# Channel attention and a non-local block on one core: layer 1 taken two steps at a time, and four smaller edits beside it

## The chip, the cores and the metric

One Trainium2 chip, of which the kernel uses one core: TensorE (PE), VectorE (DVE), ScalarE (ACT), GpSimd (POOL), and the queues that issue transfers (SyncE, SP, and GpSimd's own). The metric is the device time of one execution in microseconds (us). Everything is computed in float32 except for a few bf16 helpers, and a 512-column float32 matmul shows in the trace as two records.

## The reference

Two images of 256 channels and 64 x 64 = 4096 positions go through two layers.

```python
# layer 0, per image: attention between positions, 8 heads of 32 channels
q, k, v = split(w_qkv @ x)
scores = q^T k / sqrt(32)                 # 4096 x 4096 per head
x = w_proj @ (softmax(scores) v) + x

# layer 1, per image: a non-local block
g   = maxpool2(g_w @ x + g_b)             # 256 x 1024
th  = theta_w @ x[:64] + theta_b          # 64 x 4096
phi = maxpool2(phi_w @ x[64:] + phi_b)    # 64 x 1024
y   = softmax(th^T phi) g^T               # softmax over the 1024 pooled positions
out = batchnorm(W_w @ y + W_b) + x
```

## The kernel before

The order of stages is: q, k and v of image 0; `attend(0)`, which is layer 0's attention, in 2 quads of heads times 8 blocks of 512 positions; `project(0)`; `non_local(0)`, which is layer 1; and the same three for image 1. Softmax subtracts the true maximum of every row, so each block of scores is computed twice: once for its maxima (`ps` in layer 0, `f` in layer 1), once for the exponentials (`s` in layer 0, `f2` in layer 1, whose tile shows as `f` at L816 too). The maxima of later blocks run between the steps of the present one, one piece with each call of `advance`.

**Denominators of layer 0.** The exponentials `p` of a block are summed over its 32 key steps in three places: two heads in `sums[0]`, by GpSimd additions (L517, L526), the other two in `sums[1]` and `sums[2]`, by accumulating transfers that GpSimd issues (L523, 1 MB each). `normalize` is a generator that the code after it advances in pieces. For most blocks GpSimd folds the sums and the matmuls with `ones` (L544, tile `den`) add over the partitions. For the last block of an image, matmuls add all the pieces instead: `sums[0]`, in image 1 also `blk.last` (which VectorE accumulates, L515), and four halves of `sums[1]` and `sums[2]`. ScalarE copies `den` to `r`, VectorE takes the reciprocal (L555), and GpSimd multiplies the numerators `y` by it (L581). `project` works through eight blocks of 512 columns with four matmuls each (L646, two buffers of the pool `ps_s`), and VectorE adds the residual x, loaded by SP into `x_res`, into `y` (L653). It runs all of `normal` out before its block 4.

**Layer 1.** `ps_s` has two buffers of two PSUM banks (`scores`), `ps_m` four of one bank (`scratch`). For each block i of 512 columns, theta and the first half of phi are row-tiled matmuls (64 rows each, L683 and L684, at the same time in two parts of the array), the second half of phi is a full 128-row matmul (L687). ScalarE writes theta with its bias, VectorE pools phi. Then g follows in two halves (L703), each pooled by VectorE (L710). The recording layer `tc` may let an instruction of later code stand earlier on its engine; `tc.issue_after(x)` holds the instructions recorded under it behind x. In the built program the matmuls of `wg` (W applied to g, L725) stand between the two halves of g in blocks 1 to 7. After that come six pieces of maxima, and the loop over 8 blocks of 4 steps: `f2` (L816, two row-tiled matmuls, and at step 0 also the negated maxima, L827), exp on ScalarE (L831), then `weigh` of the step before: four full matmuls (L778) into two `scratch` banks and GpSimd's additions of p for the denominator. One piece of maxima (`f`, L746, two row-tiled matmuls and one VectorE reduce over 1024 elements, L753) follows each step. When a block's maxima are complete, GpSimd splits them into three bf16 terms (L141 to L145), TensorE turns them (`pt`, L150) and ScalarE copies them to `rows` (L161). At the end of a block `result` runs a `den` matmul (L790), reads it through ScalarE into `r` (in block 7 the reciprocal reads `den` in PSUM), takes the reciprocal, and VectorE makes z from the two y banks in four steps (L798, L801); one transfer per block stores z.

The buffers of tag `one` (six of 128 x 1024) hold p of both layers, `x_res`, `whole` and z.

Of the kernel before, what the change touches and what calls it, by code (L numbers as in the profile page):

```python
# [35 lines left out]
def conv_attention(  # L36
# [393 lines left out]
    def attend(b, y):  # L430
# [97 lines left out]
        def normalize(blk):  # L528
            theirs = [blk.sums[n][:, j] for j in range(2) for n in (1, 2)]
            if (blk.qd, blk.i) != (QUADS - 1, NI - 1):  # L530
                with tc.issue_after(added.ins):
                    nc.gpsimd.dma_start(out=blk.sums[1], in_=blk.sums[2], accum_op=ALU.add)
                yield
                theirs = [single(f"whole_{blk.name}")]
                with tc.issue_after(added.ins):
                    nc.gpsimd.tensor_add(theirs[0], blk.sums[1][:, 0], blk.sums[1][:, 1])
                yield
            den = scratch(f"den_{blk.name}")
            mine = [[blk.sums[0], *blk.last], theirs]
            for n in range(max(map(len, mine))):  # L540
                for h in range(QH):
                    those = mine[h // 2]
                    if n < len(those):
                        nc.tensor.matmul(  # L544
                            den[bass.ts(h, D), :],
                            ones[:, :D],
                            those[n][:, h % 2, :],
                            start=(n == 0),
                            stop=(n == len(those) - 1),
                        )  # L550
            r = work.tile([P, NB], F32, tag="r", name=f"r_{blk.name}", bufs=1)
# [84 lines left out]
    def project(b, y, normal, wproj_sb):  # L636
        for i in range(NI):
            if i == NI // 2:
                for _ in normal:
                    pass  # L640
            cols = bass.ts(i, NB)
            xc = load_x(b, i, single(f"x_res_{b}_{i}"))
            s = scores(f"proj_{b}_{i}")
            for o in range(NC):
                for c in range(NC):
                    nc.tensor.matmul(  # L646
                        s[:, o, :],
                        wproj_sb[:, c, bass.ts(o, P)],
                        y[:, c, cols],
                        start=(c == 0),  # L650
                        stop=(c == NC - 1),
                    )
            nc.vector.tensor_add(y[:, :, cols], s, xc)  # L653
# [4 lines left out]


    def non_local(b, y, theta_w, phi_w):  # L660
        theta = [double(f"theta_{b}_{t}") for t in range(2)]
# [14 lines left out]
        nc.sync.dma_start(out=ww_sb, in_=ww.rearrange("(o p) m -> p o m", p=P))  # L676
        for i in range(NI):
            cols, small = bass.ts(i, NB), bass.ts(i, NB // 4)
            s = scores(f"tp_{b}_{i}")
            with ExitStack() as order:  # L680
                if i:
                    order.enter_context(tc.issue_after(last_g.ins))
                nc.tensor.matmul(s[:, 0, :], theta_w, y[:CM, 0, cols], start=True, stop=True)  # L683
            nc.tensor.matmul(  # L684
                s[:, 1, :], phi_w[CM:, 0, :], y[CM:, 0, cols], start=True, stop=False
            )
            nc.tensor.matmul(s[:, 1, :], phi_w[:, 1, :], y[:, 1, cols], start=False, stop=True)  # L687
            nc.scalar.activation(
                theta[i], s[:, 0, :], AF.Identity, bias=par[:, THETA_B : THETA_B + 1]
            )  # L690
            nc.vector.tensor_reduce(
                phi[:, small].rearrange("p (r w) -> p r w", w=WW // 2),
                pooled(s[:, 1, :]),
                AX.XY,
                ALU.max,
            )
            nc.vector.tensor_scalar_add(
                phi[:, small], phi[:, small], par[:, PHI_B : PHI_B + 1]
            )
            s = scores(f"g_{b}_{i}")  # L700
            for o in range(NC):
                for c in range(NC):
                    last_g = nc.tensor.matmul(  # L703
                        s[:, o, :],
# [13 lines left out]
                )  # L718
        nc.gpsimd.tensor_sub(dphi, phi[:, 2 * P :], phi[:, : M - 2 * P])

        for t in range(M // P // 2):
            a = scratch(f"wg_{b}_{t}")
            for j in range(2):
                for c in range(NC):
                    nc.tensor.matmul(  # L725
                        a[:, bass.ts(j, C)],
# [7 lines left out]
            )  # L734

        ready = []

        def maxima1():
            for i in range(NI):
                neg = work.tile([P, NB // P, QH], F32, tag="neg1", name=f"neg1_{b}_{i}")  # L740
                nc.gpsimd.memset(neg, 0.0)
                for g in range(NB // P):
                    f = scores(f"f_{b}_{i}_{g}")
                    for h in range(2):
                        half = bass.ts(h, CM)
                        nc.tensor.matmul(  # L746
                            f[:, h, :],
                            theta[i][half, bass.ts(g, P)],
# [3 lines left out]
                        )  # L752
                    nc.vector.tensor_reduce(neg[:, g, 0:1], f, AX.XY, ALU.max, negate=True)  # L753
                    if g < NB // P - 1:
                        yield
                nc.vector.tensor_copy(neg[:, :, 2], neg[:, :, 0])
                ready.append(negate(f"l1_{b}_{i}", neg, 1))
# [5 lines left out]
        last = M // P // 2 - 1  # L763
        acc, waiting = {}, None

        def weigh(i, t, p):
            if t == 0:
# [3 lines left out]
            else:  # L771

                for j in range(2):
                    nc.gpsimd.tensor_add(acc[i][NC], acc[i][NC], p[:, j, :])  # L774
            for j in range(2):
                edge = dict(start=(t == 0 and j == 0), stop=(t == last and j == 1))
                for o in range(NC):
                    nc.tensor.matmul(  # L778
                        acc[i][o], wg[:, 2 * t + j, bass.ts(o, P)], p[:, j, :], **edge
                    )  # L780
            if t == last:
                finish.append(i)

        finish = []

        def result(i):
            cols = bass.ts(i, NB)
            z = single(f"z_{b}_{i}")
            den = scratch(f"den1_{b}_{i}")
            nc.tensor.matmul(den, ones, acc[i][NC], start=True, stop=True)  # L790
            r = work.tile([P, NB], F32, tag="r", name=f"r1_{b}_{i}", bufs=1)
            if i < NI - 1:

                nc.scalar.copy(r, den)
                den = r
            nc.vector.reciprocal(r, den)  # L796
            for o in range(NC):
                nc.vector.scalar_tensor_tensor(  # L798
                    z[:, o, :], acc[i][o], bn_scale[:, o : o + 1], r, ALU.mult, ALU.mult
                )  # L800
                nc.vector.scalar_tensor_tensor(  # L801
                    z[:, o, :], z[:, o, :], bn_shift[:, o : o + 1], y[:, o, cols], ALU.add, ALU.add
                )
            nc.sync.dma_start(out=dst[:, :, cols], in_=z)

        advance(maxes1, NB // P + 2)
        later = ready[0]()
        for i in range(NI):
            rows = later
            for t in range(last + 1):  # L810
                if t == 0:
                    s = scores(f"f2_{b}_{i}")
                for h in range(2):
                    half = bass.ts(h, CM)
                    keys = phi if t == 0 else dphi[:, 2 * P * (t - 1) :]
                    nc.tensor.matmul(  # L816
                        s[:, h, :],
                        keys[half, bass.ts(h, P)],
                        theta[i][half, :],
                        start=(t == 0),  # L820
                        stop=(t > 0),
                        skip_group_check=t > 0,
                    )
                for h in range(2):
                    half = bass.ts(h, CM)
                    if t == 0:
                        nc.tensor.matmul(  # L827
                            s[:, h, :], ones_b[half, :], rows[half, :], start=False, stop=True
                        )
                p = single(f"p1_{b}_{i}_{t}")  # L830
                nc.scalar.activation(p, s, AF.Exp)  # L831
                if waiting is not None:
                    weigh(*waiting)
                waiting = (i, t, p)
                if finish:
                    result(finish.pop())
                if t == last and i + 1 < NI:
                    later = ready[i + 1]()
                advance(maxes1)
        weigh(*waiting)  # L840
        result(finish.pop())


# [87 lines left out]
```

## Time and profile before

| | us |
|---|---|
| median of 3 runs | 3885.74 (3884.22 to 3887.61) |
| the profiled execution, whole time | 3884.94 |
| its span | 3883.1 |
| `project` of image 0, start of its first full run to the first theta matmul | 1728.43 to 1760.23 |
| layer 1 of image 0, first theta matmul to end of the last `den` | 1760.23 to 2006.1 |
| `project` of image 1 (its first two records stand at 3594.55) | 3596.61 to 3627.18 |
| layer 1 of image 1 to the end of the span | 3627.18 to 3883.1 |

A page of the profile gives each engine's busy time and share, then the chain of work that ended last, by engine and line. A row of the chain is: start, length, engine, tile, line, records. A row of the timeline is: start, length, engine, line, operation, tiles written and read, their shapes, count; in brackets how long the engine had been idle before it, and what ended the wait. Records that stand for one group overlap in time, so pace is read from starts, not from a record's length. `SPq` and `POOLq` are queues that issue transfers.

### The profile page before, as it was taken

To read this page: it belongs to the slowest core of one execution; us is meant where nothing else is said; L and a number is where in the kernel's file an instruction comes from. 1 tells how busy PE (TensorE), PEld (TensorE's weight loads), DVE (VectorE), ACT (ScalarE), POOL (GpSimd) and SP (SyncE) were. 2 spreads that over 40 slices of the span, in tenths; PEclk is the share of its full clock that TensorE was granted. 3 is DMA by queue.
4 is the path that set the end of the run, shared out by engine and by line. 5 is a ranking of instruction groups with operands and counts; after the bars stand their busy time and mean duration, and the time that the engine had idled before them with its cause. 6 is when DMAs were issued, how large, how long until landed. Compare 5 with 4: busy or idle time off the path is not lost.

```text
span 3883.1 us, 69996 instructions
## 1 busy us (share of the span) xinstructions
PE 3852.5 (99%) x27452; PEld 1361.3 (35%) x27452; DVE 2898.4 (75%) x5449; ACT 2702.5 (70%) x3386; POOL 3092.8 (80%) x1959
## 2 busy tenths in 40 slices
PE   9999999999999999999999999999999999999998
PEld 4333333333333333333333333333333333332333
DVE  5888888788888888774458888888888888884444
ACT  5787777777777787761237777777778888887121
POOL 1888899899888999891448899998999999997043
PEclk9999999999999999999999999999999999999999
DMA  1778878778888788880018888887788888889200
GB/s 58 147 167 169 171 165 170 167 166 172 167 169 165 167 167 171 170 193 15 22 40 167 168 176 168 173 171 164 162 186 170 169 169 170 169 166 187 65 17 27
DMA packets 112876, 567.31 MB, mean 146 GB/s; under 512 B 20264, under 2 KB 22568, under 8 KB 51360
## 3 DMA queue, kind: packets, MB, share of 16 engines
q0 software_dynamic: 68832, 501.25, 63.9%
q1 hardware_dynamic: 43024, 60.79, 4.6%
q8 instruction: 215, 3.52, 0.3%
q14 instruction: 117, 0.96, 0.1%
q10 hardware_dynamic: 688, 0.79, 0.1%
HBM read 51.63 MB, written 8.88 MB: 16 GB/s over the span
## 4 chain that ended last, share of the span: by engine, by line
PE 96%; DMA 2%; POOL 1%; DVE 1%; issue 0%; ACT 0%; DVEq 0%; POOLq 0%; ACTq 0%
PE s L460 27%; PE w L484 26%; PE ps L301 23%; PE y L778 6%; PE q L197 2%; PE k L197 2%; PE f L746 2%; PE v L185 2%; DMA p<-p 2%; PE f L816 1%; PE g L703 1%; PE proj L646 1%; PE den L544 1%; PE tp L687 0%; PE tp L683 0%
## 5 line engine op out<-in xcount | busy, mean ns | idle before, releaser
L517 POOL TENSOR_TENSOR p<-p,p 128x1024 f32<-128x1024 f32 x945 | 2364.1, 2502 | 276.2 <-ACT p L606 256.2
L606 ACT ACTIVATE p<-s 128x1024 f32<-128x1024 f32 x2048 | 2087.4, 1023 | 562.7 <-PE ps L301 495.6
L301 PE MATMUL ps<-k,q 32*128 32x512 f32 x6142 | 2019.0, 625 | 3.5 <-DVE r L796 1.3
L313 DVE TENSOR_REDUCE part<-ps 128x1 f32<-128x512 f32 x2046 | 1315.6, 686 | 562.6 <-PE ps L301 559.5
L484 PE MATMUL w<-p,v 128*32 128x512 f32 x8192 | 1091.0, 605 | 0.9 <-ACT p L606 0.6
L460 PE MATMUL s<-q,mid_kd 32*128 32x512 f32 x3072 | 770.2, 614 | 0.0
L328 DVE CUSTOM_DVE_ANT_0 ps<-ps,over 128x512 f32<-128x512 f32 x1025 | 706.5, 692 | 26.3 <-PE ps L301 15.1
L499 DVE TENSOR_TENSOR y<-y,w 128x512 f32<-128x512 f32 x961 | 658.1, 685 | 50.9 <-PE w L484 48.5
L301 PEld LDWEIGHTS ps<-k,q 32*128 32x128 f32 x6142 | 621.7, 183 | 27.9 <-DVE part L328 11.7
L321 ACT ACTIVATE over<-ps 128x512 f32<-128x512 f32 x961 | 569.2, 592 | 10.0 <-PE ps L301 8.0
L301 PE MATMUL ps<-kd,q 32*128 32x512 f32 x1056 | 523.5, 591 | 0.0
L460 PE MATMUL s<-q,last_kd 32*128 32x512 f32 x2048 | 508.4, 615 | 3.5 <-ACT p L606 3.5
L460 PE MATMUL s<-q,kd 32*128 32x512 f32 x2048 | 510.5, 616 | 1.2 <-ACT p L606 1.1
L301 PE MATMUL ps<-last_kd,q 32*128 32x512 f32 x904 | 444.0, 589 | 0.0
L484 PEld LDWEIGHTS w<-p,v 128*32 128x32 f32 x8192 | 161.1, 108 | 805.0 <-DVE part L313 775.4
L460 PEld LDWEIGHTS s<-q,mid_kd 32*128 32x128 f32 x3072 | 269.9, 183 | 443.5 <-ACT over L321 256.6
L523 POOL DMA_DIRECT2D p<-p x448 | 395.6, 883 | 27.8 <-ACT p L606 27.7
L460 PEld LDWEIGHTS s<-q,kd 32*128 32x128 f32 x2048 | 173.3, 183 | 301.5 <-ACT over L321 182.0
L460 PEld LDWEIGHTS s<-q,last_kd 32*128 32x128 f32 x2048 | 172.5, 183 | 283.3 <-ACT over L321 178.6
L778 PE MATMUL y<-p,kv 128*128 128x512 f32 x512 | 236.3, 605 | 0.0
L774 POOL TENSOR_TENSOR sums<-sums,p 128x512 f32<-128x512 f32 x96 | 121.3, 1264 | 100.6 <-ACT p L831 96.8
L831 ACT ACTIVATE p<-f 128x1024 f32<-128x1024 f32 x64 | 65.5, 1023 | 182.9 <-PE f L816 155.8
(121 smaller groups left out, 2810.3 us busy)
## 6 DMA issues: line engine op xcount, KB each, us to landing
p<-p POOLq DMA_DIRECT2D x478, 1024.0 KB, 7.6
x_q<-in_x_dram SPq DMA_DIRECT2D x30, 512.0 KB
x_k<-in_x_dram SPq DMA_DIRECT2D x24, 512.0 KB
x_res<-in_x_dram SPq DMA_DIRECT2D x16, 512.0 KB
out_dram<-z SPq DMA_DIRECT2D x16, 512.0 KB
r<-flat SPq DMA_DIRECT2D x120, 64.0 KB
x<-in_x_dram SPq DMA_DIRECT2D x8, 512.0 KB
last_kd<-first_kd SPq DMA_DIRECT2D x4, 256.0 KB
```

The lines of the kernel that those rows point to most:

```text
L197: nc.tensor.matmul(pq, wqk_sb[:, c, qd, 0 if what == "q" else 1, :], xc[:, c, :], start=(c == 0), stop=(c == NC - 1),)
L301: nc.tensor.matmul(ps, q[n, i][bass.ts(h, D), bass.ts(g, P)], keys[bass.ts(h, D), :], start=True, stop=True,)
L313: reduced = nc.vector.tensor_reduce(part[:, g, h, j : j + 1], ps, AX.X, ALU.max)
L321: cut = nc.scalar.activation(over, ps, AF.Relu)
L328: reduced = nc.vector.tensor_tensor_reduce(out=ps, in0=ps, in1=over, scale=1.0, scalar=LEAST, op0=ALU.add, op1=ALU.max, accum_out=part[:, ...
L460: nc.tensor.matmul(s[:, t, :], kj[bass.ts(h, D), :], q[blk.n, blk.i][bass.ts(h, D), :], start=False, stop=True, skip_group_check=j > 0,)
L484: nc.tensor.matmul(w[bass.ts(h, D), :], v[blk.n][:, keys(j), h, :], p[h // 2][:, h % 2, :], start=True, stop=True,)
L499: nc.vector.tensor_add(blk.num, blk.num, w)
L517: added = nc.gpsimd.tensor_add(blk.sums[0], blk.sums[0], p[0])
L523: sent = nc.gpsimd.dma_start(out=blk.sums[n], in_=two, accum_op=ALU.add)
L606: nc.scalar.activation(p[pair], s, AF.Exp, scale=scale)
L778: nc.tensor.matmul(acc[i][o], wg[:, 2 * t + j, bass.ts(o, P)], p[:, j, :], **edge)
```

## The change

1. Last block of layer 0's attention in each image: VectorE, not TensorE, adds up the four halves of `sums[1]` and `sums[2]` into a tile `whole`, in three additions of 128 x 1024, and in image 1 first adds `blk.last` into `sums[0]`. Four `den` matmuls remain for every block. `project` advances `normal` at its blocks 2 and 4 and runs it out at block 5.
2. Layer 1: theta and phi of all eight blocks come first, in groups of two blocks (the row-tiled matmuls of both, then the full ones of both). Then g of the eight blocks, with two pieces of maxima and one `wg` after blocks 2, 4 and 6. All these matmuls keep the order in which they are written (`product1`).
3. Two steps of the loop at a time: `f2`, two pieces of maxima, the next `f2`, then `weigh` of the two steps before. Where no maxima remain, one `weigh` stands between the two `f2`.
4. The maxima of odd pieces go to two single banks, and VectorE reduces each bank apart (512 elements each) into `most`, and then `most` into `neg`.
5. `result`: ScalarE copies the two y banks into z, and `den` and VectorE's steps follow; `weigh` calls it directly. In image 1's last block there is no copy; `den` and the reciprocal are issued before the last step's y matmuls, these go by output half, and z is stored in halves.

In the built program's order of instructions, TensorE's are otherwise those of before. On VectorE, in image 0, all three additions into `whole` stand ahead of the first `y += proj`; the second and third wait for the last accumulating transfer. In image 1 the first stands ahead of the first `y += proj`, and the other two stand between the first and the second. SP's loads of `x_res` 2 and 3 in image 0 come one buffer later, and 4 and 5 follow the loads of g_w and W_w. In g, the first matmul of each second half waits for VectorE's reduce of the first half, in both programs.

```diff
         def normalize(blk):
-            theirs = [blk.sums[n][:, j] for j in range(2) for n in (1, 2)]
...
+            else:
+                if blk.last:
+                    nc.vector.tensor_add(blk.sums[0], blk.sums[0], blk.last[0])
+                theirs = single(f"whole_{blk.name}")
+                nc.vector.tensor_add(theirs, blk.sums[1][:, 0], blk.sums[1][:, 1])
                 yield
+                for j in range(2):
+                    nc.vector.tensor_add(theirs, theirs, blk.sums[2][:, j])
+            yield
...
     def project(b, y, normal, wproj_sb):
         for i in range(NI):
-            if i == NI // 2:
+            if i in (2, NI // 2):
+                advance(normal)
+            elif i == NI // 2 + 1:
                 for _ in normal:
                     pass
...
+    def product1(*args, **kw):
+        nonlocal last1
+        last1 = tc.keep_in_program_order(nc.tensor.matmul(*args, **kw))
...
+        for i in range(0, NI, 2):
+            two = [theta_phi(i), theta_phi(i + 1)]
+            for _ in range(2):
+                for one in two:
+                    next(one)
...
-                    nc.vector.tensor_reduce(neg[:, g, 0:1], f, AX.XY, ALU.max, negate=True)
+                    for h in range(2):
+                        nc.vector.tensor_reduce(most[:, g, h : h + 1], f[h], AX.X, ALU.max)
...
+            copied = r is None
+            if copied:
+                for o in range(NC):
+                    nc.scalar.copy(z[:, o, :], acc[i][o])
+                r = denominators(i)
...
+        for i in range(NI):
+            values(i)
+            if i % 2 == 0 and i > 0:
+                advance(maxes1, 2)
+                w_values(i // 2 - 1)
+        with tc.issue_after(last1.ins):
+            rows = ready[0]()
+        for i in range(NI):
+            for u in range(0, last + 1, 2):
+                two = [step(i, u)]
+                if NB // P * i + u + LEAD1 < NI * NB // P:
+                    advance(maxes1, 2)
+                elif waiting:
+                    weigh(*waiting.pop(0))
+                two.append(step(i, u + 1))
+                if u + 2 > last and i + 1 < NI:
+                    with tc.issue_after(last1.ins):
+                        rows = ready[i + 1]()
+                if (i, u) == (0, 0):
+                    w_values(last)
+                for w in waiting:
+                    weigh(*w)
+                waiting = two
+        for w in waiting:
+            half_first = b == B - 1 and w[1] == last
+            weigh(*w, [(o, j) for o in range(NC) for j in range(2)] if half_first else None)
```

## The prediction, before the changed kernel was run

> **What bounds the kernel now.** I read the page's engine shares first, then the chain of waits from the end of image 0's attention to the start of image 1's, then the timeline at the places that the change touches, and the windows for the granted clock.
>
> ```profile
> PE 3852.5 (99%) x27452; PEld 1361.3 (35%) x27452; DVE 2898.4 (75%) x5449; ACT 2702.5 (70%) x3386; POOL 3092.8 (80%) x1959
> PE 96%; DMA 2%; POOL 1%; DVE 1%; issue 0%; ACT 0%; DVEq 0%; POOLq 0%; ACTq 0%
> ```
>
> TensorE is never idle for long, so an edit counts by what it does to TensorE's queue: work, waits, and the price of changing between row-tiled and full matmuls. The chain has all three:
>
> ```profile
> 1733.90 9.66 DMA p<-p
> 1743.60 2.77 PE den L544 x12
> 1746.37 13.93 PE proj L646 x32
> ...
> 1871.99 1.06 PE f L746 x4
> 1873.05 0.86 PE f L816 x4
> 1873.90 3.63 PE y L778 x8
> ...
> 1894.62 0.86 PE den L790 x2
> 1895.48 1.06 PE f L746 x4
> ...
> 2005.23 0.87 PE den L790 x2
> 2006.12 3.37 DVE r L796
> ```
>
> One 512-column f32 matmul is two records. A row-tiled pair (f) takes 0.86, but 1.06 when it follows a full matmul; eight y records take 3.63, where proj's pace (13.93 for 32, one change in it) makes 3.43. So each change of tiling costs 0.2. A block of layer 1 lasts 23.49 (1871.99 to 1895.48) with eight changes in it. The waits in and beside layer 1:
>
> ```profile
> 1764.92 0.70 PE L703 MATMUL g<-y,g 128*128 128x512 f32 x1 [0.78 <-DVE g L710]
> 1732.17 1.23 DVE L653 TENSOR_TENSOR y<-proj,x_res 128x1024 f32<-128x1024 f32 x1 [2.89 <-PE proj L646]
> 3595.39 1.23 DVE L515 TENSOR_TENSOR p<-p,p 128x1024 f32<-128x1024 f32 x1
> 3873.06 3.36 DVE L796 RECIPROCAL r<-den 128x512 f32<-128x512 f32 x1 [11.46 <-PE den L790]
> 3879.26 0.37 SPq L804 DMA_DIRECT2D out_dram<-z  x1
> 2010.00:2015.00 5.00, 5.00 (x24) 2.82 (x22) 4.79 (x10) 2.53 (x3) 0.00 (x0) 0.66 0.27 105
> ```
>
> The last row is a window (busy time by engine, then the clock): after TensorE had waited at 2009.54 the granted clock averaged 0.66 over 5 us, 1.7 us of TensorE time lost.
>
> **The change part by part.** All sums are against the profiled execution (span 3883.1, whole time 3884.94); the median shown, 3885.74, is 0.8 above it.
>
> *Denominators of image 0's last attention block, in `project`.* Removed: 12 of 20 den records and their waits; 1742.36 to 1746.30 was 3.94, and four quarter-column matmuls take 1.06 (the timeline's first den group, 1742.37, eight records): -2.9. Added: three VectorE adds of 128x1024, 1.23 each (row L515). What decides is where they stand in VectorE's queue. In the changed program's order they stand ahead of the first `y += proj` of image 0: the w_30 add, the first add of `whole` (waits for the accumulating transfer issued at 1726.24, 9.8 to landing: 1736.0), the w_31 add, then two adds that wait for the transfer issued at 1733.90, landing 9.66 later at 1743.56. Queued behind these are all the `y += proj` adds, and TensorE waits for them, because proj has two buffers. So: 1743.56 + 2 x 1.23 + 1.23 = 1747.3 for the first proj add. TensorE has done proj 0 and 1 by 1728.43 + 6.9 = 1735.3 and stands 12.0 where it stood not at all. Net +9.1. Bounds: the transfers of this stretch took 7.3 to 9.8, so +6.7 to +9.2; I take the one that was measured for this very transfer.
>
> *The clock after that stop.* A wait of a few us cost 1.7 at the seam between the images; here the stop is 12 us and full matmuls follow back to back. Between nothing and two such stretches (3.4); I take one and a half, +2.5.
>
> [...] The seam's row shows a drop with only 1.32 us of marked idle. [...]
>
> *The same in image 1.* The queue differs: `whole`'s first add (transfer issued 3589.69, 10.6 to landing, 3600.3), w_31, `sums += last`, the first proj add, then the two adds that wait for the last transfer:
>
> ```profile
> L523 POOL DMA_DIRECT2D p<-p x1: 856/856/856, 3594.9 to 3594.9; - x1
> DMA to landing us min/median/max: 13.3/13.3/13.3
> ```
>
> That is 3608.2. First proj add: 3600.3 + 1.23 + 0.69 + 1.23 + 1.23 = 3604.7, so proj 2 starts 1.9 late (four proj blocks ended at 3609.7, so two at 3602.8). Second: 3608.2 + 3 x 1.23 = 3611.9, so proj 3 starts at 3611.9 and not at 3608.1. Five blocks at 3.43 and den 1.06 end at 3630.1, against 3627.18: +3.0. Without any wait it would be -2.6 (den 3.64 to 1.06). SP's loads of x_res 2 to 4 now wait for later VectorE work, which leaves the transfers less company, so I take +2.0. A drop of the clock after the 3.8 us stop: 0 to 3.4, taken as half of one, +0.9.
>
> *Layer 1, each image.* Before: 1760.23 to 2006.1, 245.9. After, from the pieces above. theta and phi: four groups of two full and two row-tiled steps with two changes each, 4 x 3.83, and 0.35 for the first bank's proj add: 15.7. g: 8 x 3.43, and each second half now waits for the VectorE reduce of the first (0.78, the row above), because wg's matmuls, which stood in seven of these gaps, now stand apart: 33.7. wg 0 to 2: 5.1. Three double groups of f in between, 2.1 each: 6.3. From the first rows to the first y (pt and rows 0.22 each, four f2 and four f pairs at 0.86, wg 3 at 1.7, four changes): 9.8. Then the loop: eleven groups of four row-tiled pairs 3.63, three split ones with two f2 at 1.06, y as 13 groups of 7.06 and six of 3.63 (three pairs split), less one change in the last: 169.4 with eight den, six pt and seven rows at 0.22 each. One new wait: the second y bank of blocks 1 to 5 is the one that pt used, and ScalarE copies pt only after the exp of step 3. f2's end + 0.1 + 1.02 + 0.58 + 0.1 = 1.8, while TensorE is there after pt and one y matmul, 1.3: 0.57 x 5 = 2.9. Sum 242.9, against 245.9: -3.0, of which I take -2.7, since a loop of this length has some odd waits that no row shows. Twice: -5.4. From below: without the pt wait -6 each; from above: one more change per block and 0.2 more for each g, +2 each. The rest has cover: the new y copies (2 x 0.58 on ScalarE) end while den and f2 (1.9) run; VectorE's eight maxima of 0.69 take the place of four of 1.24 and, with the reciprocal and four z steps, fill 12 of 22.7; GpSimd's additions for den have 17 us. If such cover went, f2 would wait for exp at about 1 us a block.
>
> *Seam between the images.* The copy of den to SBUF for block 7 puts 0.65 ahead of the 3.36 reciprocal, on which VectorE's maxima wait; against that three banks come free early and the clock may stay up (1.7). -3.0 to +0.7, taken -0.7.
>
> *End.* Before, y's end at 3872.0, then den 0.9, reciprocal 3.36, four z steps of 0.7, transfer 3.84: 11.1 to 3883.1. After, den and reciprocal lie beside the last four y matmuls (3.43), so the z steps start at y's end: 2.95 + 3.84 less what half a transfer saves (0 to 1.2). Gain 3.2 to 4.5, -3.7.
>
> Sum: 9.1 + 2.5 + 2.0 + 0.9 - 5.4 - 0.7 - 3.7 = +4.7. 3885.74 + 4.7 = 3890.4, rounded to 3890. The measurement tells about 0.2% (7.8 us) from no change, so this is no change, on the slow side.
>
> **The rivals.**
> *The loop saves nothing (slower).* If a new wait takes the saved changes of tiling, layer 1 is at 245.9 again: 3895.8. Against: every buffer in the block has over 0.5 us to spare but the one counted. For: 23.25 per block rather than 23.49 is little, and from 0.2 us a block over all sixteen on, the sum passes 3893.5.
> *Image 1's stop in full (slower).* Transfer at 13.3 and two clock stretches: +1.0 + 2.5, 3893.9. For: this landing was measured. It decides with any one more us.
> *The adds hide (faster).* If VectorE's adds held nobody, project would gain 2.9 and 2.6, no clock would drop, and the sum is -15.3: 3870. The last transfer would have to land by 1735.3 - 3.7 = 1731.6, before it is issued at 1733.90. Only a different issue order on GpSimd could do that, and its order there is unchanged. *Half way (faster):* transfers at 7.3 (-2.4 and -2.0), pt's wait hidden (-5.8 in both images), no drop of the clock (-3.4): 3890.4 - 13.6 = 3876.8. Each is open, all three together are unlikely.
>
> **How the numbers follow.** Forecast 0.50 (3880 to 3893), loop 0.20, image 1's stop 0.14, adds hidden 0.06, half way 0.10. The slow cases end around 3894 to 3900, with both together at 3899; the fast ones reach 3870. Leaving out the farthest tenth on either side: 3879 to 3901. Slower by over 0.2%: the two slow cases, 0.34; faster: 0.06 and most of half way, 0.14; the same: the forecast and the rest, 0.52.
>
> **What would show it.** In image 0 VectorE idles until the transfer lands and TensorE stands some 12 us with proj waiting for `y`; the windows after it show a clock below 1. Blocks of layer 1 last about 23.2 (22.7 in the last-but-ones), y in runs of 16 records; g's second halves each wait 0.8 for VectorE. After the last y the span has 6 to 7 us left. Wrong if proj runs through (then 3870), if blocks last 23.5 or more, or if f2 waits for exp.

## The result: 0.5% slower

The changed kernel takes 3906.11 us (median of 6 runs, 3904.6 to 3909.02), the kernel before 3886.47 (6 runs, 3884.22 to 3891.18). The ratio is 1.005, 95% interval 1.0039 to 1.0061: +19.6 us, where +4.7 was forecast and the range ended at 3901. The profiled execution took 3904.64, its span is 3902.9.

The page of the changed kernel, its engine row and its chain:

```profile
PE 3842.5 (98%) x27424; PEld 1363.5 (35%) x27424; DVE 2938.2 (75%) x5536; ACT 2718.8 (70%) x3417; POOL 3102.0 (79%) x1959
PE 95%; DMA 2%; DVE 1%; POOL 1%; issue 1%; ACT 1%; DVEq 0%; ACTq 0%; POOLq 0%
```

TensorE is busy for 10 us less and the span is 20 longer, so it waits for some 30 us more. Cut at the same marks in both traces (first `proj` matmul, first theta matmul, end of an image's last y matmul, second group of weighted sums `w` of image 1), the two profiled executions compare so:

| stage, us | before | after | difference | forecast |
|---|---|---|---|---|
| project, image 0 | 31.80 | 43.13 | +11.3 | +9.1 +2.5 |
| layer 1, image 0, to the end of y | 244.99 | 245.12 | +0.1 | -2.7 |
| seam, end of y to the second `w` of image 1 | 13.07 | 16.00 | +2.9 | -0.7 |
| attention of image 1, to its first `proj` | 1576.25 | 1582.85 | +6.6 | not in the sum |
| project, image 1 | 32.63 | 34.98 | +2.4 | +2.0 +0.9 |
| layer 1, image 1, to the end of y | 244.98 | 246.03 | +1.1 | -2.7 |
| end of y to the end of the span | 10.97 | 6.16 | -4.8 | -3.7 |

In the last two rows 0.9 is only moved: `den` now stands ahead of the last y matmuls. So layer 1 gained nothing in either image, and the end gained 3.9. Each stage time here and below comes from one profiled execution of a kernel; how much a stage varies between executions of one kernel is not known.

**Project, image 0.** The timeline of the changed kernel, TensorE and VectorE:

```profile
1728.57 7.13 PE L651 MATMUL proj<-y,weights 128*128 128x512 f32 x16
1747.67 12.61 PE L651 MATMUL proj<-y,weights 128*128 128x512 f32 x24 [11.96 <-DVE y L658]
...
1736.11 3.77 DVE L540 TENSOR_TENSOR whole<-p 128x1024 f32<-128x1024 f32 x1 [8.38 <-DMA p<-p]
1744.00 2.48 DVE L543 TENSOR_TENSOR whole<-whole,p 128x1024 f32<-128x1024 f32 x2 [3.52 <-DMA p<-p]
1746.40 2.35 DVE L658 TENSOR_TENSOR y<-proj,x_res 128x1024 f32<-128x1024 f32 x2
```

VectorE waits for the first transfer (to 1736.11), adds, waits for the second (to 1744.00), adds twice, and only then comes to the first `y += proj`. TensorE stands for 11.96.

The windows of the changed kernel (length; busy time of PE, PEld, DVE, ACT, POOL; granted clock; DMA share; GB/s):

```profile
1735.00:1738.00 3.00, 0.70 (x2) 0.00 (x0) 1.89 (x1) 0.00 (x0) 3.00 (x3) 1.00 0.83 171
1738.20:1751.80 13.60, 4.13 (x5) 1.83 (x6) 6.99 (x6) 0.00 (x0) 1.85 (x2) 0.50 0.78 216
1752.00:1755.00 3.00, 3.00 (x9) 1.33 (x8) 1.22 (x1) 0.00 (x0) 0.00 (x0) 1.00 0.11 42
```

The clock is halved from 1738.2 to 1751.8; TensorE works for 4.13 of that. Its `proj` records start 0.86 apart there and 0.43 apart behind it, so the drop costs some 2.1 (an estimate, half of the 4.13).

**Project, image 1.** TensorE stands twice, for shorter:

```profile
3626.58 3.70 PE L651 MATMUL proj<-y,weights 128*128 128x512 f32 x8 [2.57 <-DVE y L658]
3632.10 7.13 PE L651 MATMUL proj<-y,weights 128*128 128x512 f32 x16 [1.82 <-DVE y L658]
```

**Layer 1.** Two second halves of g and one block's y, from the changed kernel's timeline:

```profile
1790.19 3.70 PE L668 MATMUL g<-y,g 128*128 128x512 f32 x8 [0.78 <-DVE g L731]
1794.67 3.70 PE L668 MATMUL g<-y,g 128*128 128x512 f32 x8 [0.78 <-DVE g L731]
...
1869.06 6.28 PE L668 MATMUL y<-p,kv 128*128 128x512 f32 x14 [0.44 <-ACT rows_l L161]
```

Eight records of g take 4.48 from start to start; at proj's pace they take 3.43. The wait that is marked as 0.78 costs 1.05.

**Seam.** The changed kernel's chain of waits (start, length, engine, tile, line):

```profile
2016.83 0.87 PE den L668 x2
...
2017.72 0.59 ACT r L825
...
2018.34 3.36 DVE r L827
...
2021.74 0.50 DVE part L313
2022.24 1.31 DVE z L840 x2
2023.55 1.32 DVE z L848 x2
2024.88 0.61 DVE part L313
```

The second maximum (`part`) that frees a bank for TensorE ends at 2025.49, 7.8 after `den`; the clock record shows half clock from 2024.88 for 6.83.

**Attention of image 1.** It is the same code, and 14 of its 16 blocks run at the old pace. The 6.6 arise at the starts of the other two. Counted through both images, block 24 (first of image 1's second quad) loses 3.1, block 31 (the last one) 3.2. At both an accumulating transfer lands late (block 24's first weighted sums start at 2842.76, block 31's at 3531.54, and at 2828.06 and 3513.62 in the kernel before); first the changed kernel's chain, then that of before:

```profile
2842.30 12.09 DMA p<-p
...
3530.62 9.16 DMA p<-p
```
```profile
3512.78 7.43 DMA p<-p
```

The second of the changed kernel's rows answers to the row of before, where the first has no such row: its transfer, issued at 2827.39, had landed by 2837.05, when GpSimd's next transfer was released by ScalarE. From a block's first weighted sums to the landing, block 31's transfer took 8.2 and not 6.6; the other half of its 3.2 stands with a half clock of 3.41 that follows at 3550.64. Block 24 has no such drop in this execution.

### The profile page after: what moved, and what is told of

It reads as the page before. It is cut to its first block, busy times and chain, and to the rows that moved or that the text cites. A ratio compares the mean times of both kernels' runs of the same rounds, so it can differ in the third digit from the quotient of the medians.

```text
span 3902.9 us, 70078 instructions
## 1 busy us (share of the span) xinstructions
PE 3842.5 (98%) x27424; PEld 1363.5 (35%) x27424; DVE 2938.2 (75%) x5536; ACT 2718.8 (70%) x3417; POOL 3102.0 (79%) x1959
## 4 chain that ended last, share of the span: by engine, by line
PE 95%; DMA 2%; DVE 1%; POOL 1%; issue 1%; ACT 1%; DVEq 0%; ACTq 0%; POOLq 0%
PE s L460 27%; PE w L484 26%; PE ps L301 23%; PE y L668 6%; PE f L668 3%; DMA p<-p 2%; PE q L197 2%; PE k L197 2%; PE g L668 2%; PE v L185 2%; PE proj L651 1%; PE tp L668 1%; PE den L547 1%; POOL p L517 1%; PE wg L668 0%
## 5 line engine op out<-in xcount | busy, mean ns | idle before, releaser
L301 PEld LDWEIGHTS ps<-k,q 32*128 32x128 f32 x6142 | 621.7, 183 | 27.7 <-DVE part L328 11.8
L804 POOL TENSOR_TENSOR sums<-sums,p 128x512 f32<-128x512 f32 x96 | 129.3, 1346 | 85.9 <-ACT p L879 81.0
L301 PEld LDWEIGHTS ps<-kd,q 32*128 32x128 f32 x1056 | 185.3, 184 | 22.8 <-issue 14.7
```

The costliest lines, as they stand in the source:

```text
L301: nc.tensor.matmul(ps, q[n, i][bass.ts(h, D), bass.ts(g, P)], keys[bass.ts(h, D), :], start=True, stop=True,)
```

## The experiments

Each kernel was timed against the kernel before on the same chip; a difference below is that of medians, a stage that of the profiled execution.

**1. The old denominators in the changed kernel** (`e1_old_den`).

```diff
-                for j in range(2):
-                    nc.vector.tensor_add(theirs, theirs, blk.sums[2][:, j])
...
+            mine = [[blk.sums[0], *blk.last], theirs]
+            for n in range(max(map(len, mine))):
...
-            if i in (2, NI // 2):
-                advance(normal)
-            elif i == NI // 2 + 1:
+            if i == NI // 2:
```

> The changed kernel with the denominators of the last attention block as before (TensorE multiplies all partial sums, nothing is added on VectorE, and they stand in project at block 4). Stages are read as: project = first proj matmul to first theta/phi matmul (before 31.8 and 32.6 us in images 0 and 1, changed kernel 43.1 and 35.0); attention of image 1 = its second group of weighted sums to its first proj matmul (1576.2 before, 1582.8 in the changed kernel). Theory 'stop' (VectorE's adds in front of the first y add hold TensorE): project falls to 31.8 and 32.6, no half clock is left near 1740, and the span falls by 13.7, from 3902.9 to 3889.2, if the rest stays. Rival 'clock or loads' (project is long for another reason, such as the later loads of x_res): project stays over 38. For image 1's attention: theory 'chance' (how long accumulating transfers take to land at a block's end depends on what the other queues carry just then): anywhere from 1575 to 1584, not tied to one edit; rival 'seam' (it follows from the new start of the image): 1582.8 again, since the seam is unchanged here.

Measured: +0.9 against before, ratio 1.0005 (0.9996 to 1.0014). Project of image 0 took 32.71:

```profile
1729.22 14.00 PE L646 MATMUL proj<-y,weights 128*128 128x512 f32 x32
1743.15 1.06 PE L544 MATMUL den<-p,ones 128*32 128x512 f32 x8
1745.30 2.77 PE L544 MATMUL den<-p,ones 128*32 128x512 f32 x12 [1.09 <-DMA p<-p]
```

Project of image 1 took 37.42 and missed its 32.6: VectorE waited 7.16 there for `x_res`, and the clock dropped for 3.41. The attention of image 1 took 1577.7, with the seam of the changed kernel (16.25). So the denominators alone make nearly the whole loss, and more of it than the 13.7 of the two projects.

**2. Only the new denominators in the kernel before** (`e2_only_den`): the reverse of that diff, on the kernel before.

> The kernel before with only the new denominators of the last attention block (three VectorE adds, four matmuls). Theory 'stop': project takes 43.1 and 35.0 in images 0 and 1 instead of 31.8 and 32.6, a half clock of some 13 us begins near 1738, and the span grows by 13.7 to 3896.8 from this part alone. Rival 'clock or loads': project under 38 in image 0 here, because SP's loads stand as they stood. Layer 1 stays at 245.8. Attention of image 1: 'seam' says 1576.2 as before, 'chance' says 1575 to 1584.

Measured: +18.1, ratio 1.0051 (1.0038 to 1.0064). Project took 43.29 and 34.50, with 13.65 us at half clock from 1737.5 on:

```profile
1747.41 12.42 PE L651 MATMUL proj<-y,weights 128*128 128x512 f32 x24 [12.31 <-DVE y L658]
```

Theory "stop" holds in both directions. The attention of image 1 took 1583.8, though the seam's code is that of before: the rival "seam" falls. In these two executions the slow attention came with the denominators and went with them; with one execution of each this does not rule out chance, and run 4 has the new denominators and a fast attention. The code of this attention is the same in both kernels; the edit removes TensorE instructions ahead of it and shifts it in time.

**3. g's halves for two blocks alternating** (`e3_g_pairs`).

```diff
-        def values(i):
+        def values(two):
+            s = [scores(f"g_{b}_{i}") for i in two]
             for o in range(NC):
+                for a, i in zip(s, two):
```

> The changed kernel with g computed for two blocks at a time: first halves of both, then second halves of both, so that the other block's half (1.71) stands between a half and the VectorE reduce (0.69) that frees its tile. Theory 'g waits' (each second half waits 1.05 us of TensorE time, 0.78 of it marked as idle): layer 1 of image 0 falls by 8 x 1.05 = 8.4, from 245.9 to 237.5, image 1 alike, and the span from 3902.9 to about 3886. Rival 'only the marked idle' : 8 x 0.78 = 6.2 each, span 3890.5. Rival 'VectorE takes over' (the steps of theta, phi and g queue there): less than 3 each, and f or wg wait for VectorE instead. If the lost gain of layer 1 lies in the loop instead, the loop from the first pt to the end of the denominators stays at 182.7 and g's saving comes on top, so that layer 1 is then under the 243 that was forecast.

Measured: +1.9, ratio 1.0004 (0.9996 to 1.0013), so 17.7 off the changed kernel's +19.6. Layer 1 took 236.77 and 237.68, 8.35 less in each image, which is 8 x 1.04. The first four blocks of g in its timeline run without a break:

```profile
1789.06 13.90 PE L668 MATMUL g<-y,g 128*128 128x512 f32 x32
```

**4. Image 0's last block treated as image 1's** (`e4_seam_early`).

```diff
-            if b == B - 1 and (i, t) == (NI - 1, last):
+            if (i, t) == (NI - 1, last):
...
-            if b < B - 1 or i < NI - 1:
+            if i < NI - 1:
...
-            half_first = b == B - 1 and w[1] == last
+            half_first = w[1] == last
```

> The changed kernel with image 0's last block of layer 1 treated as image 1's: denominator and reciprocal ahead of the last eight y matmuls, no copies to SBUF by ScalarE, the result stored in halves. From the end of image 0's last y matmul to the second group of weighted sums of image 1: 13.1 before, 16.0 in the changed kernel. Theory 'VectorE's queue' (den, copy 0.6, reciprocal 3.36 and four z steps of 0.66 stand ahead of the maxima that free TensorE's banks, and the wait drops the clock): the reciprocal now ends with the last y, so 4 to 5 us less, 16.0 to 11 or 12, and at most one stretch of half clock of 3.4 us is left; the span falls by 4 to 5. Rival 'clock only' (whatever is late, the first scores of an image start with gaps, and the clock drops as long): at least 6.8 us of half clock again and 2 us less or nothing. Attention of image 1: 'seam' expects it to move towards 1576 here; 'chance' makes no difference between this run and e1 or e3.

Measured: +9.0, ratio 1.0025 (1.0015 to 1.0035). The seam took 9.02, better than expected, and without any half clock. Its chain stays on TensorE:

```profile
2013.79 0.86 PE den L668 x2
2014.65 3.43 PE y L668 x8
2018.09 0.32 PE s L472 x2
2018.40 0.39 PE ps L301 x2
```

The attention of image 1 took 1577.3 in its profiled execution, which at 3892.88 is 4.7 under this kernel's median; what it takes in the others is not known.

**5. VectorE's adds behind y adds** (`e5_late_adds`).

```diff
+                with tc.issue_after(projected.ins):
+                    if blk.last:
+                        nc.vector.tensor_add(blk.sums[0], blk.sums[0], blk.last[0])
+                    nc.vector.tensor_add(theirs, blk.sums[1][:, 0], blk.sums[1][:, 1])
...
-            nc.vector.tensor_add(y[:, :, cols], s, xc)
+            projected = nc.vector.tensor_add(y[:, :, cols], s, xc)
```

> The changed kernel with its VectorE adds for the last block's denominators held behind y adds: the first two behind the y add of project block 1, the other two behind that of block 3; all else as changed. Project was 31.8 and 32.6 us before, 43.1 and 35.0 in the changed kernel. Theory 'stop' (TensorE stood only because these adds stood ahead of the y adds in VectorE's queue): now the four den matmuls (1.06) replace twenty (3.94) and nobody waits, so project takes 28.9 to 29.6 and 30.0 to 31.0, there is no half clock near 1740, and the span falls from 3902.9 by 19 to about 3884 if image 1's attention stays at 1582.8. Rival 'loads of x_res' (blocks 2 and 3 of x_res wait for buffers that GpSimd's last sums free, whatever VectorE does): project of image 0 stays over 33.

Measured: +6.8, ratio 1.002 (1.0011 to 1.0028). Project took 33.97 and 33.40: the stop of 12.0 shrank to 3.39, the clock was halved for 3.41 instead of 13.65, and both theories have a part. The stop came from the adds, but project stayed over 33 as the rival said, and the 28.9 to 29.6 of theory "stop" were missed. Its chain shows what is late next:

```profile
1731.81 2.64 POOL p L517
...
1734.46 10.12 DMA x_res<-in_x_dram
...
1744.67 1.24 DVE y L663
```

`whole` takes one of the six buffers, so `x_res` of block 2 waits until GpSimd's sum frees another, and then lands 10.12 later among the accumulating transfers.

**6. Nine small matmuls more in image 0's project** (`e6_pad`).

```diff
+            if (b, i) == (0, 2):
+                idle = scratch("idle")
+                for _ in range(9):
+                    tc.keep_in_program_order(
+                        nc.tensor.matmul(
+                            idle[:, :P], ones_b, ident_b, start=True, stop=True
+                        )
+                    )
```

> The changed kernel with nine small matmuls (128 columns, bf16, result unused) in image 0's project, where TensorE stands anyway: 18 more TensorE instructions ahead of image 1, so that its code lies there as it lay in the kernel before. In the last attention block of image 1 the kernel before lost nothing and the changed kernel 3.2 us: there the accumulating transfer issued 0.9 before the block's first weighted sums took 9.2 to land instead of 7.4, and a 16 KB fetch of TensorE's code ran at 6.2 to 7.2 after them, just as its last packets were due, where before it ran at 0.1 to 1.2. Theory 'code': with 18 more instructions the fetch falls at 0 to 1.5 again, the transfer lands in 7.4 to 8.2, and the 3.2 shrink to under 1; the span falls by some 2 to 3. Rival 'chance of the moment': the loss stays at 2.5 to 4. Project, the seam and block 24 (start of the second head group, +3.1) are as in the changed kernel in both.

Measured: +17.2, ratio 1.004 (1.0027 to 1.0054). Block 31's loss shrank from 3.2 to 0.6, and the transfer that took 9.16 landed in 7.65:

```profile
3533.54 7.65 DMA p<-p
```

What changed is when 16 KB of code were fetched; they are taken for TensorE's, since adding TensorE instructions alone moved the fetch. In the changed kernel's transfers between 3537.6 and 3538.9 there are two packets, the code and the last small one of the accumulating transfer:

```profile
DMA packets 2, 0.02 MB, mean 13 GB/s; under 512 B 1, under 2 KB 1, under 8 KB 1
## 3 DMA queue, kind: packets, MB, share of 16 engines
q8 instruction: 1, 0.02, 4.7%
q0 software_dynamic: 1, 0.00, 0.1%
```

The code ran from 6.2 to 7.2 after the block's first weighted sums, and the small packet ended at 7.2 with it. With the nine matmuls the code came at 0.1 to 1.4. So "code" came out as expected for block 31. The twelve profiled executions fit, but for one: where the fetch began 6.2 to 6.4 after block 31's first weighted sums (the changed kernel and runs 2, 3, 5, 7 and 8) the transfer landed in 9.1 to 9.2, and where it began at 0 to 0.6 (the kernel before and runs 1, 6, 9 and 10) in 7.3 to 7.7. Run 4, with the fetch at 6.3, landed in 7.6. Block 24 stayed slow (4.0), as expected, and this execution spent 10.2 us at half clock at the seam.

**7. The weights of g and W loaded after x_res** (`e8_g_late`).

```diff
-        nc.sync.dma_start(out=gw_sb, in_=gw.rearrange("(o p) m -> p o m", p=P))
+        with tc.issue_after(loaded.ins):
+            nc.sync.dma_start(out=gw_sb, in_=gw.rearrange("(o p) m -> p o m", p=P))
```

> The changed kernel with the loads of g's and W's weights (two of 256 KB) put behind the loads of x_res in SP's queue, so that in image 1 they come some 780 us later. In block 24 of the attention (first block of image 1's second head group) the changed kernel lost 3.1 us against before: the copy of last_kd, issued 0.12 after an accumulating transfer, overtook it and landed in 2.3 us, and x_q and these weights followed 8 us earlier than before and ran beside the next accumulating transfer, which took 12.1 instead of 9.7 to land. Theory 'g collides': without these two loads the transfer lands in 9 to 10.5, block 24 costs at most 1 more than before, image 1's attention falls from 1582.8 to 1579 to 1580.5, and the span by 2 to 4. Rival 'overtaking alone': the copy's place decides, block 24 still costs 2 to 4 more than before. Project, seam and layer 1 stay.

Measured: +15.6, ratio 1.0035 (1.0023 to 1.0048). Block 24 cost 0.7 over before and block 31 still 3.2; the attention took 1580.65. The transfer of block 24:

```profile
2844.24 8.72 DMA p<-p
```

Here the copy of `last_kd` did not overtake, so this run alone does not part the two theories. SP's queue in the changed kernel, for comparison with the next paragraph (x_q waits for the copy, which was issued at 2836.79):

```profile
2839.13 0.40 SPq L88 DMA_DIRECT2D x_q<-in_x_dram  x1
2840.93 0.40 SPq L687 DMA_DIRECT2D g<-in_gw_dram  x1
2841.38 1.31 SPq L688 DMA_DIRECT2D g<-in_ww_dram  x1
```

Over the twelve profiled executions the copy was released within 2.4 us whenever SP issued it at most 0.12 after GpSimd's transfer or just ahead of it (the changed kernel and runs 2, 3, 5, 6 and 9), and after 8.1 to 10.8 us whenever it came 0.21 to 0.39 after (the kernel before and runs 1, 4, 7, 8 and 10). With the early copy and the loads of g, block 24's transfer landed in 11.8 to 12.2 and the block lost 2.9 to 4.2 against before; with the late copy it landed in 8.7 to 9.5 and the block lost 0.7 at most. With the early copy and no such loads (run 9 below) it landed in 9.63, and the block lost 1.8 with a half clock of 3.41 in it (runs 2, 3, 6 and 7 have one there too). So the early copy costs most by letting the loads of g in ahead of the transfer. That rests on one run, and no kernel moved the copy alone.

**8. All together** (`e7_all`): edits 3, 4, 5 and 7 on the changed kernel.

> All together on the changed kernel: VectorE's adds behind the y adds, g's halves for two blocks alternating, image 0's last block with its denominator ahead of the last y matmuls, the weights of g and W loaded after x_res. If each part does what its own run showed or is expected to show: start 1728.6, project 28.9, layer 1 237.0, seam to the second weighted sums 9.0, attention 1578, project 30.0, layer 1 237.7, end 6.1: span 3855, that is 28 under before (3883.1). Rival 'each saving brings another wait': 3865 or more, with layer 1 over 240, project over 32, or more half clocks.

Measured: -18.3, ratio 0.9952 (0.9939 to 0.9964). Layer 1 took 237.6 and 237.7, the seam 9.02, project 35.1 and 34.6, the attention 1581.5 (block 31 lost 4.7, with 6.83 us at half clock). The span, 3871.0, is the rival's.

**9. The same with the old denominators** (`e9_old_den_rest`): edits 1, 3, 4 and 7.

> The changed kernel with the denominators of the last attention block as before (TensorE multiplies the partial sums), g's halves for two blocks alternating, image 0's last block with its denominator ahead of the last y matmuls, and g's and W's weights loaded after x_res. Theory 'stop and loads' (whatever VectorE adds there, the new form takes one more buffer, so x_res of block 2 comes late: project took 34.0 and 33.4 even with the adds held back, against 31.8 and 32.6 before): here project takes 31.8 to 32.8 and 32.6 to 34, layer 1 237.5 in both images, seam 9.0, attention of image 1 1576 to 1578 (block 24 and block 31 each cost at most 1 more than before), end 6.1: span 3859 to 3863, that is 8 to 12 under the one with VectorE's adds held back and all the rest (3871.0). Rival 'no more than that one': 3867 or more.

Measured: -18.7, ratio 0.9953 (0.994 to 0.9965); span 3866.3. Project took 32.8 and 35.2, the attention 1579.8. That span lies 0.7 below the rival's bound and over the theory's range; the median of this kernel's five spans is 3867.5, the rival's. Against before, runs 8 and 9 differ by 0.4, far inside their intervals, so with the adds held back no difference between the two forms of the denominators is shown. The attention missed its 1576 to 1578: block 24 lost 1.8 and block 31 1.9, each with a half clock of 3.41, though the code was fetched early (0.1) here.

**10. Both edits for image 1's attention** (`e10_pad_g_late`): edits 6 and 7 on the changed kernel.

> The changed kernel with both edits for image 1's attention: nine small matmuls more in image 0's project, and g's and W's weights loaded after x_res. Alone, the first brought block 31's extra time over before from 3.2 to 0.7, the second block 24's from 3.1 to 1.0. Theory 'two places, two causes': both here, so image 1's attention takes 1577 to 1578.5 (1576.2 before, 1582.8 changed) and the span is some 4 to 6 under the changed kernel's 3902.9 unless the clock drops more often. Rival 'chance of the moment': one of the two places costs over 2 again.

Measured: +11.9, ratio 1.0032 (1.0021 to 1.0043). The attention took 1576.7, 0.4 over before. Block 31's transfer:

```profile
3529.22 7.30 DMA p<-p
```

Both places are within 0.3 of before, as "two places, two causes" expected. What mended block 24 is not settled by it, since the copy of `last_kd` came late here too (list under run 7). The span of the profiled execution, 3902.1, missed: project of image 1 took 38.6 with 6.83 us at half clock.

## Why the prediction was wrong, point by point

The sum of the parts was +4.7 and the span grew by 19.7. Of the 15 between them, 6.6 is the attention of image 1, which the sum left out; 5.7 is layer 1, where the wait in g was priced too low (4.3 of it); and 3.6 is the seam. The two projects and the end were sized right to within 1.

- *Denominators of image 0*: right. proj 2 was forecast at 1747.3 after a stop of 12.0, and started at 1747.67 after 11.96.
- *The clock after that stop*: right in time, 2.5 forecast and some 2.1 lost. The drop lasted four stretches of 3.41, but TensorE worked in little more than one of them.
- *The same in image 1*: right for the waits, 2.57 and 1.82, +2.4 in all against +2.0. The +0.9 for the clock did not come in this execution; runs 2, 4, 6 and 10 have a drop there.
- *Layer 1*: wrong, -5.4 forecast and +0.3 measured (without the moved `den`). The step that failed is "g: 8 x 3.43, and each second half now waits ... (0.78 ...): 33.7". It took 8 x 4.48 = 35.8. Everywhere else I had worked from the starts of records, here I added idle time as marked to a pace. Experiment 3 puts the price of one such wait at 1.04. The rest was near: theta and phi 15.8 (forecast 15.7), from the first `pt` to the last `den` 182.8 (182.1), the new wait for the `rows` copy 0.44 as marked (0.57), and a block 23.36 (23.25). The bound "+2 each" does not come out of its own terms: 0.2 for each of eight blocks and 0.2 for each of eight g add 3.2 to -3.0, which makes +0.2 each. The measurement, +0.1 and +0.2, stands at that bound.
- *Seam*: wrong, -0.7 forecast and +2.9 measured. That "three banks come free early and the clock may stay up" bought nothing: ScalarE's copy of 0.59 and then VectorE's queue (reciprocal, two maxima around four z steps) set the end, and the clock was down for 6.83 instead of 3.41. Experiment 2 shows 14.34 for the old code with a drop of 6.83, so 1.3 of the 2.9 is the longer drop and 1.7 the new order.
- *End*: right, -3.9 against -3.7.
- *What was missing*: the attention of image 1, +6.6, the largest miss. "The rest has cover" was said of the edited stages, and unedited code was costed at nothing without being named. In experiment 6 the landing of block 31's transfer moved with the time at which 16 KB of code, taken for TensorE's, were fetched: 9.16 with the fetch at 6.2, 7.65 with it at 0.1. Run 4 stands against it, 7.6 with the fetch at 6.3. For block 24 the twelve executions tie the landing to an order of issues within some 0.2 us; that is a correlation without exception, not a test. Both had moved.

Terms: 11.3 + 2.4 + 0.3 + 2.9 + 6.6 - 3.9 = 19.6 of the span's 19.7. Of the rivals, "the loop saves nothing" came true for the time of layer 1 but not by its mechanism: the gain of the loop was there and g gave it back.

What stays open: how much of the attention's 6.6 an average execution has; why the copy of `last_kd` overtakes the accumulating transfer when it is issued close behind it (no kernel moved only that issue), and why in experiment 4 block 31 lost only 0.6 although the code was fetched at 6.3 as in the changed kernel.

## What to carry to other kernels

Before moving an addition to an idle engine, write down that engine's queue: what matters is what stands behind the addition while it waits for its transfer, and which buffer its result takes from a later load. Price a wait by the starts of the instructions around it, not by the idle time marked ahead of one. And look at the places in unedited code where a chain runs through several transfers with nothing to spare: a few instructions more or fewer in an earlier stage can be enough to shift what meets there (nine small matmuls in experiment 6, and block 31's loss went from 3.2 to 0.6).

## What the runs showed of the hardware

**The clock.** Over the twelve profiled executions (mean granted clock 0.995 to 0.999) the granted clock fell to half and rose again 35 times inside the span, each time for 3.41 us or two, three or four times that: in the changed kernel at 1738.17 for 13.65, at 2024.88 for 6.83 and at 3550.64 for 3.41, in the kernel before at 2011.23 for 3.41. In the 3.41 us before a fall TensorE's records covered 0 to 67%; before these four they covered 0.94, 1.99, 2.24 and 2.09 us. In three of the 35 these 3.41 us were empty; in the other 32 no idle stretch in the 14 us ahead was longer than 3.11 (2.46, 1.17, 1.59 and 1.32 ahead of the four). Here are one window of the changed kernel at the seam and three neighbouring ones at block 31 (columns as above):

```profile
2021.47:2024.88 3.41, 1.99 (x8) 0.68 (x8) 3.41 (x7) 0.79 (x1) 0.00 (x0) 1.00 0.00 0
3547.23:3550.64 3.41, 2.24 (x12) 0.76 (x16) 0.46 (x1) 3.00 (x4) 3.23 (x2) 1.00 1.11 226
3550.64:3554.05 3.41, 3.41 (x16) 0.52 (x9) 1.82 (x2) 0.88 (x1) 2.24 (x2) 0.50 0.59 120
3554.05:3557.46 3.41, 3.41 (x32) 1.17 (x32) 0.69 (x1) 2.80 (x4) 1.22 (x1) 1.00 1.14 231
```

TensorE was busy for 1.99 and 2.24 of 3.41, and the next window ran at half clock. What brings about a fall is not shown by these rows.

**Code and transfers.** Nine small matmuls more, eighteen TensorE instructions with their weight loads, in a stage 1800 us earlier, took 2.6 us from an attention block. The transfer landed in 7.65 instead of 9.16 when a 16 KB fetch of code no longer met its end, and the half clock that followed was gone too. Run 4, where the fetch met it and the transfer landed in 7.6, shows that the meeting alone does not decide. In the changed kernel the last small packet of the transfer ended with the code, both at 7.2 after the block's first weighted sums; whether the one held the other up, and which engine carried either, is not shown by the rows of experiment 6.
